# Rope moves of three query groups split over two DMA queues

## The chip, the core and the metric

The kernel runs on one core of a Trainium2 chip. The metric is the device time of one execution, in microseconds. A core has TensorE (PE in the profile), VectorE (DVE), ScalarE (ACT), GpSimd (POOL) and SyncE (SP); SyncE only issues DMAs here, and ScalarE can issue them too, from its own instruction stream.

## What is computed

Two layers over an input of 16 x 256 x 256 floats. Each layer normalises its input, computes a sequence mixer and a gate, and adds their product. In the first layer the mixer is a linear recurrence and the gate a feed-forward network. The second layer, in which the change lies, has attention with 16 heads and a routed low-rank gate:

```python
q = (x @ Wq).reshape(B, S, N_HEADS, QK_DIM)            # 128 nope + 64 rope
q = jnp.concatenate([q_nope, apply_rope(q_rope)], axis=-1)
kv = x @ Wkv_a                                         # 64 latent + 64 rope
c_kv = c_kv * rsqrt(mean(c_kv * c_kv) + RMS_EPS) * kv_norm_w
k = jnp.concatenate([k_nope, broadcast(apply_rope(k_rope))], axis=-1)
scores = jnp.einsum('bqhd,bkhd->bhqk', q, k) * scale
attn = softmax(where(tril, scores, min))
out = jnp.einsum('bhqk,bkhd->bqhd', attn, v) @ Wo
x = x + out * silu(routed_lora_ffn(xn))
```

The projection of the latent keys is folded into the queries' weights, so a head's key is the 64 latent numbers and the 64 rope numbers of a token, 128 partitions in all.

## The kernel before

The second layer works through 8 chunks of 512 tokens (two batch entries). A chunk has 4 groups of 4 heads, and each group is done once for each of the two batch entries: 8 units a chunk, 64 units in all. Unit `i` uses query group `i // 2`, and there are 32 groups. The order of the work is written out by hand, and a helper class (line 53, so that nearly every row of the profile has L53) keeps it on each engine.

*Scores.* `score_pack(u, 0..2)` multiplies the queries of a unit, `qg`, with the keys `kT` for eight blocks of 32 queries, in three packs that use three PSUM banks (`sc`) in turn. VectorE masks and takes the maxima, ScalarE takes the exponentials into `pr`, GpSimd divides by the sums (`normalise`).

*Probabilities.* They must be transposed before they meet the values. `turn` transposes them on VectorE in 32 x 32 blocks into `turned`; `send` writes them to a DRAM buffer `far` with four DMAs; one or two units later `fetch` reads them back as `pT` with one DMA. `far` and `pT` have three buffers each, `turned` two. `values(u)` multiplies `pT` with the latent rows into `av`, which ScalarE copies to `attT`.

*Queries.* While unit `i` runs, the queries of a group ahead are made: group `n = (i + 2) // 2` at even `i`, `(i + 3) // 2` at odd `i`. `query_mm` has four matmul steps into `pq`; `query_mul` (VectorE) and `query_rot` (GpSimd) apply the rotation and leave the result in `qrot`, which has one buffer; `query_lat` (ScalarE) writes the latent half, partitions 0 to 63, of `qg`. The rope half lies in `qrot` with the heads on the partitions and must come to partitions 64 to 127 of `qg`: `query_move(n)` does that with eight DMAs, two halves of the rotation by four heads, each of 32 partitions. `qg` has two buffers. The first score matmul of unit `2n` waits for all eight, and the next group's `query_rot` cannot write `qrot` before they are done.

*SyncE's queue.* `fetch`, `send` and `query_move` are all issued by SyncE, in the order of the program. At an even unit `i` that is `fetch(i - 2)`, then `send(i - 1)`, then `query_move(n)`; only at `i = 2` the moves stand ahead of the send. At an odd unit it is `fetch(i - 2)` and `send(i - 1)`. `fetch` waits for its `send` to have landed, so SyncE stands there for some time in every unit. [...]

*Last units.* The probabilities of the last two units do not go through DRAM: TensorE transposes them (`turn_here`).

In the loop, shortened to the calls that matter here:

```python
if 2 <= i:
    fetch(units[i - 2])
score_pack(u, 0)
...                       # turn(w, 1), turn(w, 2), query_mm, query_lat
score_pack(u, 1)
if i == 2:
    query_move(n)
turn(w, 0); send(w)       # w is unit i - 1
if not odd:
    if n is not None and i != 2:
        query_move(n)
    values(units[i - 4]); values(units[i - 3])
score_pack(u, 2)
...                       # odd: query_mm, query_mul, query_rot, query_lat
```

## Time and profile before

| | us |
|---|---|
| median of 3 runs | 921.33 (920.73 to 922.28) |
| profiled execution | 921.71 |
| its span | 919.9 |
| TensorE busy | 905.2 (98%) |
| VectorE busy | 666.4 (72%) |
| GpSimd busy | 570.6 (62%) |
| ScalarE busy | 465.8 (51%) |

The span is the time from the first to the last instruction in the profile, and the execution's own time holds it and what lies around it. The mean granted clock of TensorE over the execution was 0.996 of full speed. The attention layer begins at about 285 us and fills the rest. Over the whole execution SyncE issued 248 sends, 62 read-backs and 256 moves; in the profile they read `far<-turned`, `pT<-far` and `qg<-qrot`. Engine rows marked "q" (SPq, ACTq) are instructions that issue DMAs. A row of the timeline gives start, length, engine, line, operation, tiles and the number of instructions run together, and in brackets the idle time just before it with what ended it.

### The profile page before, as it was taken

To read this page: it belongs to the slowest core of one execution; us is meant where nothing else is said; L and a number is where in the kernel's file an instruction comes from. 1 tells how busy PE (TensorE), PEld (TensorE's weight loads), DVE (VectorE), ACT (ScalarE), POOL (GpSimd) and SP (SyncE) were. 2 spreads that over 40 slices of the span, in tenths; PEclk is the share of its full clock that TensorE was granted. 3 is DMA by queue.
4 is the path that set the end of the run, shared out by engine and by line. 5 is a ranking of instruction groups with operands and counts; after the bars stand their busy time and mean duration, and the time that the engine had idled before them with its cause. 6 is when DMAs were issued, how large, how long until landed. Compare 5 with 4: busy or idle time off the path is not lost.

```text
span 919.9 us, 17382 instructions
## 1 busy us (share of the span) xinstructions
PE 905.2 (98%) x5426; PEld 695.4 (76%) x5426; DVE 666.4 (72%) x2018; ACT 465.8 (51%) x1529; POOL 570.6 (62%) x885
## 2 busy tenths in 40 slices
PE   8999999999999899999999999999999999999998
PEld 7768898987767567777777777777777777777776
DVE  6876687664688779668967866896786689677562
ACT  3335555654336545645644564564466456446541
POOL 1228697777355537686586767648676764866541
PEclk9999999999999999999999999999999999999999
DMA  9730000000025777777776777777677777767771
GB/s 280 232 115 1 1 2 1 1 2 1 1 32 106 201 203 184 203 186 186 178 210 160 208 194 192 189 178 207 159 209 206 181 190 178 205 160 211 206 224 42
DMA packets 196412, 134.00 MB, mean 146 GB/s; under 512 B 142112, under 2 KB 186976, under 8 KB 196320
## 3 DMA queue, kind: packets, MB, share of 16 engines
q1 hardware_dynamic: 194192, 128.68, 53.3%
q0 software_dynamic: 1152, 3.67, 1.2%
q8 instruction: 44, 0.72, 0.3%
q10 hardware_dynamic: 976, 0.53, 0.2%
q14 instruction: 48, 0.39, 0.1%
HBM read 63.11 MB, written 52.95 MB: 126 GB/s over the span
## 4 chain that ended last, share of the span: by engine, by line
PE 90%; DVE 3%; DMA 2%; SPq 2%; POOL 1%; issue 1%; ACT 0%; POOLq 0%; DVEq 0%; ACTq 0%
PE pq L53 22%; PE sc L53 14%; PE po L53 10%; PE av L53 9%; PE r L53 7%; PE f L53 7%; PE ph L53 5%; PE pf L53 5%; PE pg L53 4%; PE pm L53 2%; SPq L53 2%; PE pkv L53 1%; PE tp L53 1%; DMA qg<-qrot 1%; PE py L53 1%; PE pb L53 1%
## 5 line engine op out<-in xcount | busy, mean ns | idle before, releaser
L53 ACT ACTIVATE pr<-sc,nm 128x256 f32<-128x256 f32 (+7 forms) x512 | 189.7, 381 | 240.3 <-DVE sr L53 152.2
L53 POOL TENSOR_SCALAR pr<-pr,sr 128x256 f32<-128x256 f32 (+7 forms) x512 | 192.1, 394 | 190.0 <-DVE sr L53 184.1
L53 PEld LDWEIGHTS sc<-kT,qg 128*128 128x128 f32 x1024 | 157.6, 191 | 62.3 <-issue 40.3
L53 PE MATMUL sc<-kT,qg 128*128 128x256 f32 (+7 forms) x1024 | 176.1, 306 | 5.7 <-DMA qg<-qrot 4.4
L53 DVE TENSOR_REDUCE nm<-sc 128x1 f32<-128x256 f32 (+7 forms) x512 | 127.5, 301 | 6.6
L53 DVE STREAM_TRANSPOSE turned<-pr 128x512 f32<-128x512 f32 x186 | 123.2, 687 | 9.6 <-POOL pr L53 8.7
L53 PE MATMUL pq<-xnT,wlat 128*128 128x512 f32 x256 | 124.1, 608 | 0.0
L53 PE MATMUL pq<-xnT,wrope 128*128 128x512 f32 x256 | 120.2, 593 | 0.0
L53 ACT ACTIVATION_READ_ACCUMULATOR pr<-sc,nm 128x1 f32 x512 | 104.3, 204 | 0.0
L53 DVE TENSOR_TENSOR sc<-sc,kmask 128x96 f32<-128x96 f32 (+1 forms) x192 | 45.5, 237 | 64.9 <-PE sc L53 63.9
L53 PE MATMUL av<-pT,row 128*64 128x256 f32 (+1 forms) x1024 | 90.9, 329 | 0.5 <-DMA pT<-far 0.5
L53 POOL TENSOR_TENSOR qrot<-qmul,qmul 128x512 f32<-128x512 f32 x64 | 83.0, 1317 | 8.0 <-POOL pr L53 2.9
L53 PEld LDWEIGHTS av<-pT,row 128*64 128x64 f32 x1024 | 64.1, 137 | 24.3 <-issue 1.6
L53 DVE TENSOR_TENSOR qmul<-pq,rot_q 128x512 f32<-128x512 f32 x128 | 80.7, 672 | 0.1
L53 ACT ACTIVATE qg<-pq 64x512 f32<-64x512 f32 x128 | 75.4, 589 | 5.4 <-PE pq L53 4.7
L53 PEld LDWEIGHTS pq<-xnT,wlat 128*128 128x128 f32 x256 | 46.0, 192 | 32.0 <-issue 32.0
L53 PEld LDWEIGHTS pq<-xnT,wrope 128*128 128x128 f32 x256 | 45.7, 191 | 32.4 <-issue 32.1
L53 PEld LDWEIGHTS po<-wout,attT 128*128 128x128 f32 x416 | 58.4, 191 | 9.5 <-issue 4.9
L53 PE MATMUL po<-wout,attT 128*128 128x128 f32 (+1 forms) x416 | 64.5, 308 | 0.0
L53 POOL TENSOR_TENSOR rs<-ve,mhalf 128x4 f32<-128x4 f32 (+1 forms) x17 | 16.8, 986 | 51.3 <-DVE ve L53 37.0
L53 PE MATMUL ph<-xnT,p1T 128*128 128x256 f32 (+1 forms) x128 | 44.3, 503 | 0.8 <-DVE xnT L53 0.8
L53 POOL TENSOR_TENSOR attT<-attT,attT 128x512 f32<-128x512 f32 x36 | 45.0, 1270 | 0.0
(226 smaller groups left out, 1505.0 us busy)
## 6 DMA issues: line engine op xcount, KB each, us to landing
far<-turned SPq DMA_DIRECT2D x248, 192.0 KB, 4.3
pT<-far SPq DMA_DIRECT2D x62, 768.0 KB, 5.0
qg<-qrot SPq DMA_DIRECT2D x256, 64.0 KB, 2.3
x<-in_x_dram SPq DMA_DIRECT2D x7, 512.0 KB, 9.3
out_dram<-x POOLq DMA_DIRECT2D x12, 256.0 KB, 4.9
wqn_wo<-in_wq_nopeT_dram SPq DMA_DIRECT2D x4, 512.0 KB, 4.9
wqn_wo<-in_Wo_dram SPq DMA_DIRECT2D x4, 512.0 KB, 6.1
p2T<-in_proj2T_dram SPq DMA_DIRECT2D x2, 512.0 KB, 7.2
```

What stands on the lines that cost most here:

```text
L53: r = getattr(self.engine, name)(*args, **kw)
```

## The change

At three units, `i` = 2, 4 and 60, the eight moves of a group (2, 3 and 31, that is the third, the fourth and the last) are taken from their place and split. The four moves of the first half are issued by SyncE at the start of the unit, in front of `fetch`. The four of the second half are issued by ScalarE, behind the exponentials of pack 1 and in front of whatever ScalarE does next. All other groups stay as they were.

```diff
-    def query_move(n):
+    def query_move(n, halves=(0, 1), e=sp):
         q = groups[n]
-        for r in range(2):
+        for r in halves:
             for h in range(G):
-                sp.dma_start(
+                e.dma_start(
                     q.qg[64 + 32 * r : 96 + 32 * r, :, h, :],
                     q.rot[32 * h : 32 * h + 32, r, :].rearrange("p (a q) -> p a q", q=32),
                 )
...
+    SOON = (2, 4, LAST - 4)
...
+        if i in SOON:
+            query_move(n, (0,))
         if 2 <= i:
             fetch(units[i - 2])
         score_pack(u, 0)
...
-        if i == 2:
-            query_move(n)
+        if i in SOON:
+            query_move(n, (1,), ac)
         if w:
...
         if not odd:
-            if n is not None and i != 2:
+            if n is not None and i not in SOON:
                 query_move(n)
```

## The prediction

> **What bounds the kernel now.** I read the page's busy shares first, then TensorE's waits, the timeline of each such wait, and SyncE's (SP's) queue ahead of it. The busy shares and TensorE's waits:

> ```profile
> PE 905.2 (98%) x5426; PEld 695.4 (76%) x5426; DVE 666.4 (72%) x2018; ACT 465.8 (51%) x1529; POOL 570.6 (62%) x885
> ```
> ```profile
> PE sc L53 <- DMA qg<-qrot: 4.4, 2, 3.5
> PE sc L53 <- ACT pr L53: 1.3, 1, 1.3
> PE av L53 <- DMA pT<-far: 0.5, 1, 0.5
> ```

> TensorE is the bound; in the attention layer it has few waits, and one of 3.5 us is the largest. On the timeline of TensorE (start, length, idle before it) these waits lie at three places that the change could touch, and a fourth that it leaves:

> ```profile
> 321.68 1.05 PE L53 MATMUL sc<-kT,qg 128*128 128x256 f32 x4 [3.47 <-DMA qg<-qrot]
> 322.57 3.35 PE L53 MATMUL pq<-xnT,wlat 128*128 128x512 f32 x4
> ...
> 881.40 1.87 PE L53 MATMUL sc<-kT,qg 128*128 128x256 f32 x10 [1.26 <-ACT pr L53]
> ...
> 885.24 1.52 PE L53 MATMUL av<-pT,row 128*64 128x256 f32 x16 [0.52 <-DMA pT<-far]
> ```

> The first is unit 6, which opens query group 3: its scores need the eight rope moves of that group, and the last landed at 321.27. The 881.40 row is unit 62, which opens group 31; the profile names ScalarE as releaser, but its exps were done at 880.86 and the last move of group 31 landed at 880.99, so it is the moves here too. 885.24 is values(59), released by its read-back. The fourth, 0.95 us at 380.60 (group 6), is left alone.

> Now SP's queue, which carries read-back (pT<-far), sends (far<-turned) and moves (qg<-qrot):

> ```profile
> 309.91 0.34 SPq L53 DMA_DIRECT2D pT<-far  x1
> 310.29 3.30 SPq L53 DMA_DIRECT2D far<-turned  x4
> 313.71 5.93 SPq L53 DMA_DIRECT2D qg<-qrot  x8
> 319.74 0.56 SPq L53 DMA_DIRECT2D pT<-far  x1
> ...
> 869.76 0.34 SPq L53 DMA_DIRECT2D pT<-far  x1
> 870.23 3.24 SPq L53 DMA_DIRECT2D far<-turned  x4
> 873.89 5.46 SPq L53 DMA_DIRECT2D qg<-qrot  x8
> 879.45 0.56 SPq L53 DMA_DIRECT2D pT<-far  x1
> ```

> Group 3's qrot was ready at 306.87 (GpSimd's timeline), yet its moves began at 313.71: SP was held until 309.9 by the landing of send(2), then issued a read-back and four sends. Group 31 likewise: ready at 866.22, moved from 873.89. Eight moves hold SP for 5.93 us, 0.63 us each, and land 2.3 us after issue (page, DMA issues). The queue's order makes the stall, not the transfers.

> **What the stall costs.** More than it shows. The granted clock in the stretch is below full:

> ```profile
> 301.00:318.00 17.00, 17.00 (x98) 11.30 (x96) 14.07 (x46) 9.83 (x40) 10.16 (x20) 1.00 0.77 225
> 318.00:341.00 23.00, 19.53 (x104) 13.16 (x104) 14.67 (x56) 10.01 (x37) 8.34 (x18) 0.93 0.75 188
> 341.00:361.00 20.00, 19.97 (x108) 14.21 (x108) 18.13 (x58) 13.24 (x54) 13.47 (x25) 1.00 0.72 172
> ```

> 0.93 over 23 us is one interval of 3.41 us at half speed (322.83 to 326.24), right behind the 3.47 us of idleness. The four pq matmuls there took 3.35 us; the same four take 1.96 at 316.25. With the six score matmuls behind them (1.25 instead of 1.08) that is about 1.6 us. [...]

> **The change, part by part.** At i = 2, 4 and 60 (groups 2, 3 and 31) four of eight moves go to the head of SP's queue, and four to ScalarE's queue behind pack 1's exps.

> *Removed from SP.* Four moves, 4 x 0.67 = 2.7 us of SP a site (interval of unhindered issues: 0.66 to 0.67). The other four run while SP used to wait: at i = 4 from 306.9, at i = 60 from 866.2.

> *Added to ScalarE.* Four issues a site. No row shows a move issued by ScalarE while it works. Below: its five issues of loads at the start, 0.33 to 0.48 us. Above: a move held up on SP, 1.24 us (at 314.34). I take 0.67, SP's interval for the same tile form, so 2.7 us a site. ScalarE then reaches pack 2's exps late: pack 1 ended at 307.93 (i = 4), pack 2 began at 309.27. Queued behind the moves are values' copy to attT (307.81, 0.6 us), pack 2's exps and one activation for the key/value chunk, and on them wait VectorE and GpSimd. ScalarE is 51% busy and the score ring is three banks deep, which hides the exps from TensorE; VectorE's work on the chunk moves from 310.6 to about 314.2, and the transposes behind it by up to 3.6 us.

> *i = 2.* SP's halves 290.0 to 292.6; ScalarE's from 295.4, landed about 300. fetch(0) goes from 290.98 to about 297.7 and lands by 303, needed at 304.9. fetch(1) goes from 303.0 to about 304.6, lands 309.5, needed at 311.6. Nothing gained or lost; the cover is 2 us.

> *i = 4.* ScalarE's moves 309.7 to 312.3 (behind the attT copy or the last exps), SP's by 314. qg_3 is complete at about 316; TensorE would want it at 318.05. **The stall and its clock dip go: 5.1 us, locally.** But fetch(2) slides from 309.91 to about 314.0, fetch(3) from 319.74 to 321.05, fetch(4) from 327.22 to 328.15, and send(5) stays at 328.8 against 328.73. So SP reaches group 4's moves when it did before, and they land at about 339.7 against 339.76. Unit 8 opens with them; in the trace it starts at 340.30, with TensorE free at 340.16. TensorE, now 5 us early, waits: 2.5 us at values(3), whose read-back lands at 326.2, and the rest at unit 8. **What remains of 5.1 us is what group 4's moves gain: 0.1 us at 0.67 us an issue, 1.3 us at 0.47.** I take 0.5.

> *i = 60.* SP's halves 865.2 to 870.3 (one waits for send(58)'s landing at 869.6), ScalarE's 869.8 to 872.4. fetch(58) slides from 869.76 to 872.15, but its probabilities are needed only at 883.2. Group 31 lands at about 875, so the 1.26 us at 881.40 go; fetch(59) goes at 879.25 instead of 879.45 and lands at 884.35 (5.1 us in flight), so values(59) starts at 884.45 against 885.24. **0.8 us**, with bounds 0.2 and 1.8 (1.26 + 0.52). This is near the end: no later move takes it back.

> Sum: 0.5 + 0.8 = **1.3 us**. The profiled execution took 921.71 us (span 919.9), which becomes 920.4; it lies 0.4 above the median of 921.33, which becomes **920.0**.

> [...] The row says 0.63 us of issue against 2.3 us of transfer, eight in a row: 5 us of a queue is not small. [...]

> **The rivals.** (0.2%, 1.84 us, is about what a measurement of this kernel can tell from no change.)

> *More is kept.* ScalarE issues in 0.47 us, or the moves land before SP looks for them, and group 4 comes 1.3 us earlier; with 0.8 to 1.3 at the end, 2.1 to 2.6 us: 919.0. For it: every issue that ScalarE has in this trace lies below 0.5. Against: those were into an idle chip. Were nothing given back, 5.1 + 1.8 = 6.9 us would be the most; unit 8's moves exclude that.

> *All is given back.* The read-backs slide, unit 8 takes all, values(59) keeps its time: 921.3. For it: 339.76 against 340.16 at group 4, and pT<-far releasing 885.24. Against: fetch(59) stood behind eight moves.

> *Slower: ScalarE's issues jam.* One mechanism: SP's fetch(2) waits for ScalarE's four moves, and SP's later issues slide with them. The four intervals count twice on the way to unit 8: in fetch(2)'s start, and in the exps and transposes behind the moves, on which send(5) waits. Eight intervals of 0.67 us leave unit 8 where it was, so it moves by 8 intervals less 5.4 us, an estimate. With 0.8 at the end, nothing is lost up to 0.77 us an issue, and 0.2% from about 1.0. At the jammed row's 1.24 us unit 8 is 4.5 us late, less 0.8: 3.7 us, 925.0. For it: far and pT packets fill the queues at 75% DMA share, and 1.24 to 1.61 us do occur. Against: they occur once in eight, not four times.

> **How the numbers follow.** Central case (0.4 to 1.84 us gained) 0.38; more kept 0.37; given back, within 0.4 us, 0.12; jam, 0.13 beyond 0.2%. Faster by over 0.2% is 'more kept' and a little of the central case, 0.39; within 0.2% 0.48; slower 0.13. The range runs from 918.3 (3 us gained: 1.3 with all of the end's 1.8) to 922.8 (a jam of 0.85 us an issue and noise of 0.9, the spread of the three runs); the jam's far end and a larger gain are left out, 2 in 10.

> **What would show it.** Right: no qg wait at unit 6 and clock 1.00 from 318 to 341; a new wait of 2 to 3 us at values(3), by pT<-far; unit 8 waiting on qg; SP's fetch(2) at about 314, waiting for a qg<-qrot landing; no wait at unit 62, and values(59) 0.8 us nearer the stage's start; ScalarE's moves about 0.67 us each. Wrong: a qg wait at unit 6 still there, ScalarE's moves at over 1 us, a half-clock interval at values(3) or unit 8 (one costs 1.6 us), or units after 8 that keep over 2 us.

## The result

The changed kernel took 925.76 us (median of 13 runs, 923.48 to 930.19) against 921.55 us (13 runs, 919.41 to 925.29) for the kernel before: ratio 1.0044, interval 1.0032 to 1.0056. It is 4 us slower where 1.3 us of gain were forecast. The execution that was profiled first, at 923.48 us, is the fastest of the 13, with a span of 921.7 us (before: 921.71 us and 919.9 us), so its trace shows 1.8 us of the 4. A second profiled execution of the same kernel, at 926.29 us, is nearer to the median; both are shown.

TensorE's waits, first profile, then the second:

```profile
PE av L53 <- DMA pT<-far: 5.1, 2, 3.1
PE sc L53 <- DMA far<-turned: 2.1, 1, 2.1
```
```profile
PE av L53 <- DMA pT<-far: 4.8, 2, 3.4
PE sc L53 <- DVE sr L53: 3.2, 1, 3.2
PE sc L53 <- DMA far<-turned: 1.8, 1, 1.8
```

The 4.4 us on qg<-qrot are gone, and in their place stand waits for read-backs and two new waits of scores. On TensorE's timeline, first profile:

```profile
303.16 1.05 PE L53 MATMUL sc<-kT,qg 128*128 128x256 f32 x4 [2.10 <-DMA far<-turned]
...
319.79 0.97 PE L53 MATMUL sc<-kT,qg 128*128 128x256 f32 x4
...
327.85 1.87 PE L53 MATMUL av<-pT,row 128*64 128x256 f32 x16 [3.10 <-DMA pT<-far]
...
881.75 1.79 PE L53 MATMUL sc<-kT,qg 128*128 128x256 f32 x10
...
887.01 1.52 PE L53 MATMUL av<-pT,row 128*64 128x256 f32 x16 [2.02 <-DMA pT<-far]
```

Unit 6 (319.79) and unit 62 (881.75) start without a wait: the moves do come early enough. But unit 4 (303.16) now waits 2.10 us, values(3) 3.10 us, and values(59) 2.02 us instead of 0.52. The releaser named at 303.16 is wrong: a score matmul needs no far<-turned. The trace has group 2's last move, on ScalarE's queue, landing at 302.73, and the name went to a send that landed beside it, at 303.17.

Where the time went, as the start of the same matmul in the two first profiles (each from its own span's start; differences of unrounded times):

| matmul | before | after | difference |
|---|---|---|---|
| unit 4, first score | 301.50 | 303.16 | +1.66 |
| unit 6, first score | 321.68 | 319.79 | -1.90 |
| unit 6, pack 1 (the half-clock stretch is gone) | 325.71 | 322.31 | -3.40 |
| values(3) | 328.24 | 327.85 | -0.39 |
| unit 8, first score | 340.30 | 343.10 | +2.79 |
| unit 62, first score | 881.40 | 881.75 | +0.35 |
| values(59) | 885.24 | 887.01 | +1.77 |

Between values(3) and unit 8 the changed kernel loses 3.2 us with no wait at all. The windows show why (the last three figures of a row are the granted clock, the busy share of the DMA engines and their GB/s):

```profile
318.00:324.00 6.00, 6.00 (x30) 3.77 (x31) 5.93 (x19) 3.92 (x17) 2.68 (x6) 1.00 0.68 212
324.00:332.00 8.00, 4.90 (x37) 3.98 (x34) 3.08 (x12) 3.73 (x12) 2.68 (x5) 0.80 0.67 220
332.00:345.00 13.00, 13.00 (x55) 9.53 (x55) 9.48 (x37) 4.67 (x20) 2.92 (x8) 0.86 0.77 208
```

The clock ran at half speed from 328.88 for 6.83 us (granted clock 0.50 up to 335.71), twice the 3.41 us of before; the sixteen pm matmuls there took 3.97 us instead of 2.10. In the second profile the half-clock stretch (granted clock 0.84 from 341 to 352) comes after unit 8, which there waits 3.20 us for group 4's moves:

```profile
344.62 1.56 PE L53 MATMUL sc<-kT,qg 128*128 128x256 f32 x4 [3.20 <-DVE sr L53]
```

The last of these moves landed at 344.07; the profile names VectorE. So the wait that left unit 6 turned up at values(3) and unit 8, and its clock loss came with it, once or twice over.

SyncE's and ScalarE's queues, first profile:

```profile
293.78 0.71 ACTq L53 DMA_DIRECT2D qg<-qrot  x1
294.53 0.64 ACTq L53 DMA_DIRECT2D qg<-qrot  x1
295.21 1.32 ACTq L53 DMA_DIRECT2D qg<-qrot  x2
```
```profile
289.39 2.61 SPq L53 DMA_DIRECT2D qg<-qrot  x4
296.18 0.35 SPq L53 DMA_DIRECT2D pT<-far  x1
...
310.18 4.20 SPq L53 DMA_DIRECT2D qg<-qrot  x4
314.49 0.55 SPq L53 DMA_DIRECT2D pT<-far  x1
315.09 2.26 SPq L53 DMA_DIRECT2D far<-turned  x4
322.95 0.34 SPq L53 DMA_DIRECT2D pT<-far  x1
```

The same queue before, at i = 2:

```profile
290.98 0.34 SPq L53 DMA_DIRECT2D pT<-far  x1
...
303.02 0.34 SPq L53 DMA_DIRECT2D pT<-far  x1
303.47 2.35 SPq L53 DMA_DIRECT2D far<-turned  x4
```

ScalarE's issues at i = 2 take 0.64 to 0.71 us, as assumed. The read-backs are late: fetch(0) at 296.18 instead of 290.98, fetch(2) at 314.49 instead of 309.91, fetch(3) at 322.95 instead of 319.74. Fetch(0) goes out 0.08 us after ScalarE's first move has landed (296.10); in the trace the two share a completion counter.

### The profile page after: what moved, and what is told of

Its sections match the earlier page's. It is cut to its first block, busy times and chain, and to the rows that moved or that the text cites. A ratio compares the mean times of both kernels' runs of the same rounds, so it can differ in the third digit from the quotient of the medians.

```text
span 921.7 us, 17371 instructions
## 1 busy us (share of the span) xinstructions
PE 906.0 (98%) x5426; PEld 697.6 (76%) x5426; DVE 665.8 (72%) x2018; ACT 466.0 (51%) x1529; POOL 570.8 (62%) x885
## 4 chain that ended last, share of the span: by engine, by line
PE 94%; DMA 3%; DVE 1%; SPq 0%; ACT 0%; issue 0%; POOL 0%; ACTq 0%; POOLq 0%
PE pq L53 23%; PE sc L53 15%; PE po L53 10%; PE av L53 9%; PE r L53 7%; PE f L53 7%; PE ph L53 5%; PE pg L53 5%; PE pf L53 5%; PE pm L53 2%; PE pkv L53 2%; PE tp L53 1%; DMA far<-turned 1%; DMA pT<-far 1%; PE py L53 1%; PE pb L53 1%
## 5 line engine op out<-in xcount | busy, mean ns | idle before, releaser
L53 POOL TENSOR_SCALAR pr<-pr,sr 128x256 f32<-128x256 f32 (+7 forms) x512 | 191.8, 393 | 190.6 <-DVE sr L53 184.4
L53 ACT ACTIVATE pr<-sc,nm 128x256 f32<-128x256 f32 (+7 forms) x512 | 189.8, 381 | 233.1 <-DVE sr L53 145.9
L53 PEld LDWEIGHTS sc<-kT,qg 128*128 128x128 f32 x1024 | 158.5, 192 | 57.8 <-issue 40.9
L53 PE MATMUL sc<-kT,qg 128*128 128x256 f32 (+7 forms) x1024 | 176.8, 307 | 2.2 <-DMA far<-turned 2.1
L53 DVE TENSOR_REDUCE nm<-sc 128x1 f32<-128x256 f32 (+7 forms) x512 | 127.7, 301 | 6.6
L53 DVE STREAM_TRANSPOSE turned<-pr 128x512 f32<-128x512 f32 x186 | 123.4, 688 | 9.4 <-POOL pr L53 9.2
L53 PE MATMUL pq<-xnT,wlat 128*128 128x512 f32 x256 | 122.7, 602 | 0.0
L53 PE MATMUL pq<-xnT,wrope 128*128 128x512 f32 x256 | 120.2, 593 | 0.0
L53 ACT ACTIVATION_READ_ACCUMULATOR pr<-sc,nm 128x1 f32 x512 | 104.4, 204 | 0.0
L53 PE MATMUL av<-pT,row 128*64 128x256 f32 (+1 forms) x1024 | 91.5, 330 | 5.1 <-DMA pT<-far 5.1
L53 DVE TENSOR_TENSOR sc<-sc,kmask 128x96 f32<-128x96 f32 (+1 forms) x192 | 45.8, 238 | 62.6 <-PE sc L53 61.4
L53 POOL TENSOR_TENSOR qrot<-qmul,qmul 128x512 f32<-128x512 f32 x64 | 83.5, 1324 | 7.1 <-DVE qmul L53 2.8
L53 PEld LDWEIGHTS av<-pT,row 128*64 128x64 f32 x1024 | 64.3, 137 | 29.2 <-DVE turned L53 3.3
L53 DVE TENSOR_TENSOR qmul<-pq,rot_q 128x512 f32<-128x512 f32 x128 | 80.9, 674 | 0.1
L53 ACT ACTIVATE qg<-pq 64x512 f32<-64x512 f32 x128 | 75.4, 589 | 4.3 <-PE pq L53 3.5
L53 PEld LDWEIGHTS pq<-xnT,wrope 128*128 128x128 f32 x256 | 45.7, 191 | 32.4 <-issue 32.1
L53 PEld LDWEIGHTS pq<-xnT,wlat 128*128 128x128 f32 x256 | 45.7, 191 | 31.6 <-issue 31.6
L53 PEld LDWEIGHTS po<-wout,attT 128*128 128x128 f32 x416 | 58.4, 191 | 9.5 <-issue 5.1
L53 PE MATMUL po<-wout,attT 128*128 128x128 f32 (+1 forms) x416 | 64.5, 308 | 0.0
L53 POOL TENSOR_TENSOR rs<-ve,mhalf 128x4 f32<-128x4 f32 (+1 forms) x17 | 16.8, 986 | 51.0 <-DVE ve L53 37.3
L53 POOL TENSOR_TENSOR attT<-attT,attT 128x512 f32<-128x512 f32 x36 | 45.0, 1270 | 0.0
L53 PE MATMUL ph<-xnT,p1T 128*128 128x256 f32 (+1 forms) x128 | 44.1, 501 | 0.8 <-DVE xnT L53 0.8
```

The source lines that it names most:

```text
L53: r = getattr(self.engine, name)(*args, **kw)
```

## The experiments

Each difference is against the changed kernel. "Undone" means that a group goes as in the kernel before.

**The changed kernel again**, no edit.

> The changed kernel once more, for a second profile. In its first profile the span grew by 1.8 us, put together from: 2.1 us of wait at unit 4 (group 2's last move on ScalarE's queue landed at 302.7), minus the 3.5 us wait of unit 6, plus 3.1 us at values(3) (read-back) and a half-clock interval of 6.8 us instead of 3.4 us, minus 1.3 us at unit 62 and 1.5 us more at values(59). Theory (three places add up, and each is as deterministic as the queue order): the same waits in the same places, each within 0.5 us, time 925 to 927. Rival (the median's 4 us is something the first profile did not catch): other or larger waits than these.

Measured: ratio 1.0040 (1.0025 to 1.0056), median 925.71 us. The waits of unit 4 (1.78) and values(3) (3.35) lie within 0.4 us of the first profile, that of values(59) (1.43) is 0.6 us shorter. Unit 8's 3.20 us are new, and the final shift is 4.6 us instead of 1.8. The other places are as in the first profile, but the size of the wait at unit 8 and the place of the half-clock stretch differ from execution to execution, and that is what the first profile did not catch.

**One site at a time.**

```diff
-    SOON = (2, 4, LAST - 4)
+    SOON = (2,)              # only_third
+    SOON = (4,)              # only_fourth, group 2 undone
+    SOON = (LAST - 4,)       # only_last, group 2 undone
```

> Only the third group (i = 2) is split over the queues; groups 3 and 31 go as in the kernel before. Theory A: the last ScalarE move lands with the read-back's packets at about 302.7, unit 4 waits 2.1 us, SyncE's queue is 1.6 us later from then on, unit 6 keeps its wait of 3 to 3.5 us: plus 1.6 to 2.5 us, 923 to 924. Theory B: the 2.1 us are absorbed by the wait of unit 6, which shrinks to about 1.5 us: 921 to 921.8.

> Only the fourth group (i = 4) is split; group 2 goes whole in front of the send as in the kernel before, group 31 in its old place. Theory A: without the 1.7 us that unit 4 brings along, fetch(3) goes out at about 321 and values(3) waits 2 to 2.5 us, one half-clock interval or none, unit 8 within 1 us of before: 920.3 to 922. Theory B: the loss lies here whatever group 2 does: values(3) waits 3 us, two half-clock windows, 923.5 to 925.

> Only the last group (i = 60) is split. Theory A (the read-back of unit 59 is later because fetch(58) stood behind ScalarE's moves): the 1.3 us at unit 62 go, values(59) waits 1.5 to 2 us more: plus 0 to 0.5 us, 921.3 to 922. Theory B (as forecast, once the queue does not come late from earlier units): minus 0.8 us, 920.7.

Measured: only_third 1.0040 (1.0028 to 1.0052), only_fourth 1.0015 (1.0002 to 1.0028), only_last 0.9990 (0.9976 to 1.0004). **The third group alone, the site I had costed at nothing, loses about as much as all three changes together** (1.0040 against 1.0044); with the fourth group's 1.0015 the parts don't add up place by place, since in the whole change unit 6 no longer waits for a late group 3. In only_third unit 4 waits 1.92 us, and unit 6 waits on top of that what it waited before:

```profile
303.10 1.05 PE L53 MATMUL sc<-kT,qg 128*128 128x256 f32 x4 [1.92 <-DMA far<-turned]
...
323.23 1.94 PE L53 MATMUL sc<-kT,qg 128*128 128x256 f32 x4 [3.34 <-DMA qg<-qrot]
```

so theory B, that unit 6's wait would absorb it, falls: group 3's moves come later by the same amount. The loss of 3.7 us is more than theory A's 1.6 to 2.5: the profiled execution also had a longer half-clock stretch (the three groups of matmuls from 323.23 to 329.58 took 1.94, 3.62 and 1.28 us; at full speed they take 0.97, 1.88 and 0.98). Of its 3.7 us, 1.6 stand at unit 4 and 1.7 come between units 4 and 20, where that stretch is. In only_fourth the stall of unit 6 is gone, but values(3) waits 3.71 us and unit 8 another 1.85: the waits are those of theory B, with one half-clock stretch instead of its two windows (2.58 and 1.42 us for two groups of matmuls that take 1.52 and 0.85 at full speed, and full speed again at 331.41).

**The third group, three ways.**

```diff
 # third_sync_only: the second half on SyncE, at the same place
-            query_move(n, (1,), ac)
+            query_move(n, (1,))
 # third_read_first: fetch in front of SyncE's half
+        if 2 <= i:
+            fetch(units[i - 2])
         if i in SOON:
             query_move(n, (0,))
-        if 2 <= i:
-            fetch(units[i - 2])
 # third_three: ScalarE issues heads 1 to 3 alone; query_move takes the heads too
-    def query_move(n, halves=(0, 1), e=sp):
+    def query_move(n, halves=(0, 1), e=sp, heads=range(G)):
...
             query_move(n, (0,))
+            query_move(n, (1,), sp, (0,))
...
-            query_move(n, (1,), ac)
+            query_move(n, (1,), ac, (1, 2, 3))
```

All three with `SOON = (2,)`.

> Only the third group is split in time, as in only_third, but the second half is issued by SyncE too, at the same place of the program (behind fetch(0), in front of the send). Theory A: the moves follow the read-back in one queue, so fetch(0) waits for nobody and goes out at 292; the last move lands at about 299; unit 4 has no wait: 921 to 922. Theory B (taking SyncE's first halves in front of the read-back is what costs): unit 4 or unit 6 waits more than before, 923 to 925.

> Only the third group is split, as in the run only_third, but at i = 2 the read-back fetch(0) is issued in front of SyncE's four moves instead of behind them; ScalarE still issues the other four. Theory A (the 4 us of only_third come from ScalarE's last move and a read-back being issued at the same moment, 295.9 and 296.2 us, so that the move lands with the read-back, 6.7 us later): fetch(0) goes out at about 290, no move is issued beside it, ScalarE's moves land 2.3 us after issue, unit 4 has no wait, 921 to 922. Theory B (a move on ScalarE's queue is slow in itself, or it delays ScalarE): unit 4 waits again, 923.5 to 925.5.

> Only the third group is split, as in only_third, but ScalarE issues three moves instead of four and SyncE five at the head of unit 2. Theory A (the read-back starts when ScalarE's first move has landed, 2.3 us after its issue; three issues of 0.68 us are done by then, four are not, and the one in the making lands with the read-back): all three land 2.3 us after issue, unit 4 has no wait, the 2.1 us go; 921.5 to 923. Theory B (moves on ScalarE's queue land late because of the traffic of that moment, however many they are): the last lands with the read-back again at about 302.5, unit 4 waits about 2 us, 924 to 926.

Measured: third_sync_only 0.9998 (0.9985 to 1.0011), third_read_first 1.0009 (0.9995 to 1.0022), third_three 1.0024 (1.0011 to 1.0036). Third_three settles what happens at unit 4. ScalarE's three moves all land 2.2 to 2.4 us after issue (the fourth of only_third took 6.68, landing 0.24 us after the read-back that SyncE issued 0.29 us behind it), and unit 4 has no wait. But the kernel is still 2.4 parts in a thousand slower, outside theory A's time: fetch(0) waits for ScalarE's first move as before (landed at 296.35, fetch(0) at 296.42), and unit 6 now takes all of it:

```profile
324.25 1.94 PE L53 MATMUL sc<-kT,qg 128*128 128x256 f32 x4 [6.48 <-DMA qg<-qrot]
```

So the late move at unit 4 is only where the loss first shows. Its root is SyncE's chain: from unit 4's first score (301.06), fetch(1) goes out 3.34 us later and fetch(2) 10.63 us later, where before these were 1.52 and 8.41. With the second half on SyncE (third_sync_only) the read-back doesn't wait for ScalarE:

```profile
289.63 2.61 SPq L53 DMA_DIRECT2D qg<-qrot  x4
292.40 0.50 SPq L53 DMA_DIRECT2D pT<-far  x1
292.94 2.73 SPq L53 DMA_DIRECT2D qg<-qrot  x4
295.78 4.33 SPq L53 DMA_DIRECT2D far<-turned  x4
302.74 0.34 SPq L53 DMA_DIRECT2D pT<-far  x1
```

and no loss can be measured: fetch(1) is at 302.74 (before: 303.02). The early half is harmless at i = 2; SyncE's wait for ScalarE is not. Third_read_first lies between: fetch(0) goes out in time and unit 4 doesn't wait, but SyncE's fourth move goes out at 298.77, once ScalarE's first has landed (298.76), so that four moves hold the queue for 7.17 us, and unit 6 waits 4.38 us.

```profile
292.19 7.17 SPq L53 DMA_DIRECT2D qg<-qrot  x4
```

**The fourth group, three ways.**

```diff
 # fourth_read_first: fetch in front of SyncE's half, as above
 # fourth_sync_head: all eight at the head, on SyncE
-            query_move(n, (0,))
+            query_move(n)
...
-            query_move(n, (1,), ac)
 # fourth_gpsimd: all eight on GpSimd at the later place, none at the head
-            query_move(n, (0,))
...
-            query_move(n, (1,), ac)
+            query_move(n, (0, 1), gp)
```

All three with `SOON = (4,)` and group 2 undone.

> Only the fourth group is split, as in only_fourth, but fetch(2) stands in front of SyncE's four moves. Theory A (only_fourth loses because fetch(2) waits for ScalarE's moves, 314.5 instead of 309.9, and every later read-back and send slides by 3 us): fetch(2) at 309.9, fetch(3) at about 320, group 3 complete before 318, no wait at unit 6, at most 1 us at values(3), unit 8 as before: 920 to 921.3. Theory B (ScalarE's own late exps and copies, which hold VectorE's transposes for 3.6 us, cost the time): unit 8 or values(3) waits over 2.5 us again, 922.5 to 924.

> Only the fourth group is changed: all eight moves are issued by SyncE at the head of unit 4, none by ScalarE. Theory A (the loss is the order of SyncE's queue, whichever engine issues the moves): fetch(2) slides to about 312.5, fetch(3) to 320.5 or later, values(3) waits 1 to 2 us, unit 8 about as before: 920.5 to 922. Theory B (ScalarE's share is the loss): no wait over 1 us at values(3) and unit 8, 919.5 to 920.5.

> Only the fourth group is changed: all eight moves are issued by GpSimd at unit 4, behind the normalising of pack 2; SyncE and ScalarE issue none of them, and GpSimd's DMAs have completion counters of their own. Theory A (the time lost at i = 4 is all in SyncE's chain of read-back, send and read-back, which moves in front of it or on shared counters push back): fetch(2) stays at 309.9, send(3) lands by 317.5, fetch(3) goes out at 317.5 instead of 319.7, group 3 is complete by about 317, unit 6 and values(3) wait less than 1 us together, unit 8 comes 1 to 4 us earlier: 917.5 to 920. Theory B (the transfers themselves, in whatever queue, or GpSimd's issuing at over 1 us each, are the limit): unit 6 or values(3) waits over 2 us, 921 to 923.

Measured: fourth_read_first 1.0006 (0.9994 to 1.0017), fourth_sync_head 1.0001 (0.9987 to 1.0014), fourth_gpsimd 1.0003 (0.9991 to 1.0016). None gains. To compare the executions, times are counted here from unit 4's first score matmul, in us:

| kernel | fetch(2) | fetch(3) | group 3 landed | unit 6 | values(3) | unit 8 |
|---|---|---|---|---|---|---|
| before | 8.41 | 18.24 | 19.77 | 20.18 | 26.74 | 38.80 |
| only_fourth | 12.05 | 20.40 | 13.47 | 16.55 | 25.22 | 40.81 |
| fourth_read_first | 10.21 | 19.81 | 17.01 | 17.14 | 25.09 | 40.38 |
| fourth_sync_head | 11.19 | 19.82 | 12.82 | 16.55 | 25.05 | 39.22 |
| fourth_gpsimd | 8.58 | 19.42 | 17.93 | 18.06 | 24.34 | 39.58 |

Unit 6 comes 2 to 3.6 us earlier in each, and unit 8 in none. These are single executions. In four others, in which SyncE alone issues groups 2 and 3 and group 3 has its old place (third_sync_only, only_last, only_last_again, last_sync_only), fetch(3) lies at 18.28 to 18.44 and unit 8 at 38.73 to 39.71. So fetch(3) is late in all four changed kernels, by 1.2 to 2.2 us, whoever issues the moves, but unit 8 is clearly later only in the two with moves on ScalarE. And unit 8 isn't earlier where the half-clock stretch is missing: only_last has none (its four pq matmuls at 322.53 take 1.88 us, 3.35 before), and there unit 8 waits 1.40 us and starts at 38.73 all the same.

With moves on ScalarE the counters delay fetch(2). In only_fourth and fourth_read_first the last part of send(2) shares a counter with fetch(1) and goes out only when fetch(1) has landed (308.83 after 308.82; 307.59 after 307.57). In only_fourth the send takes 4.81 us to issue instead of 2.35, and SyncE's moves start behind it:

```profile
304.33 4.81 SPq L53 DMA_DIRECT2D far<-turned  x4
309.41 4.81 SPq L53 DMA_DIRECT2D qg<-qrot  x4
```

In fourth_read_first that part lands at 311.33 and fetch(2) follows at 311.35. So its lateness is no case of theory B, ScalarE's late exps.

Fourth_gpsimd takes the moves out of SyncE's queue and off its counters, and fetch(2) is on time. (GpSimd's DMAs have counters of their own: in the trace of before its 16 use eight that no DMA of SyncE or ScalarE uses. The eight of the prediction are shared by SyncE and ScalarE, not by all engines.) Yet send(3) lands late all the same, since fetch(2) took 8.14 us to land instead of 5.05, and GpSimd's moves 6.7 us (median) instead of 2.3. Their issues took 0.65 to 0.91 us, not over 1. The waits, 1.35 us at unit 6 and 1.24 at values(3), fit neither theory; the time fits theory B. The profiled execution, 925.24 us, was the slowest of its twelve (median 922.88). The DMA issues of that kernel, in the window from 303 to 325:

```profile
pT<-far SPq DMA_DIRECT2D x3, 768.0 KB, 5.0
far<-turned SPq DMA_DIRECT2D x12, 192.0 KB, 5.2
qg<-qrot POOLq DMA_DIRECT2D x8, 64.0 KB, 6.7
```

**DMAs in flight together landed later in these runs (that fetch(2) 8.14 us after its issue instead of 5.05), and the moves are no small matter there.** In the changed kernel ScalarE's queue (q10) is nearly a meter for them. Its row in the DMA queues of the whole execution, before and after:

```profile
q10 hardware_dynamic: 976, 0.53, 0.2%
q10 hardware_dynamic: 7312, 1.32, 0.8%
```

So twelve moves cost 0.6% of 921.7 us, an estimate of 0.46 us of all 16 engines each (from rounded shares), 3.7 us for a group. That is what the packets took, not a measured delay of what stands behind them: fetch(3) came 1.2 to 2.2 us late. GpSimd's queue (q0) packs the same bytes otherwise, eight moves in 256 packets where ScalarE's take 528 each:

```profile
q0 software_dynamic: 1152, 3.67, 1.2%
q0 software_dynamic: 1408, 4.20, 1.5%
```

(before, then fourth_gpsimd). So that run shows that moves from another queue hold up a read-back, not what a move on SyncE's queue costs. Nor is the delay a constant: a read-back with moves close behind it in SyncE's queue took 5.28 us (fourth_read_first), 5.44 (before, i = 2), 6.44 (third_sync_only) and 8.00 (last_sync_only). What decides is open.

In the old order the moves ran in the shade of a send that had to land anyway: send(3) landed at 316.9, moves were issued from 313.71 to 319.64, fetch(3) followed at 319.74.

Theory B of fourth_read_first has some room still behind fetch(2): unit 8 is later (40.81 and 40.38) in both kernels with moves on ScalarE than in fourth_sync_head (39.22). ScalarE's late exps and the counters are not separated there.

**The last group.**

```diff
 # last_sync_only: SOON = (LAST - 4,), group 2 undone, second half on SyncE
-            query_move(n, (1,), ac)
+            query_move(n, (1,))
```

> Only the last group (i = 60) is split in time: first half in front of fetch(58), second half behind it and in front of the send, all eight issued by SyncE. Theory A (the gain of only_last comes from the order alone; the read-backs have slack there): unit 62 has no wait, fetch(58) goes out at about 870.5 by the clock of before, values(59) is no later: ratio 0.998 to 0.9995. Theory B (the gain needs the second queue): unit 62 or values(59) waits as before or longer: 0.9995 to 1.002.

> The run only_last once more, beside last_sync_only, for a narrower interval and a second profile. If its gain is real: minus 0.5 to 1.2 us, unit 62 without a wait, values(59) waiting 1 to 1.5 us. If it was noise: within 0.3 us of before.

Measured: last_sync_only 1.0028 (1.0011 to 1.0046), only_last_again 1.0014 (1.0000 to 1.0028). With only_last's 0.9990 the two runs of the same kernel lie on either side of no change; its effect on the whole isn't resolved, and it isn't shown to beat the kernel before. Locally both profiles look like the forecast: against before, unit 62 starts 1.4 us sooner after unit 61, and values(59) gives 0.68 and 0.28 us of it back. But that is not shown to be the change: from unit 60's first score to values(59) it takes 20.69 and 20.22 us here, 21.43 before, and 20.05 to 21.92 in the eight other profiles that leave group 31 in place. The rows of the first:

```profile
879.25 1.79 PE L53 MATMUL sc<-kT,qg 128*128 128x256 f32 x10
...
883.69 1.52 PE L53 MATMUL av<-pT,row 128*64 128x256 f32 x16 [1.20 <-DMA pT<-far]
```

Last_sync_only goes against theory A, and its time lies beyond theory B's range: here the second queue does help. Part of the loss is a half-clock stretch at values(59): its sixteen av matmuls took 2.83 us instead of 1.52. With SyncE alone, four moves follow fetch(58) closely, fetch(58) takes 8.0 us to land, send(59) stretches over 5.16 us, and values(59) waits 3 us longer than before:

```profile
870.78 0.34 SPq L53 DMA_DIRECT2D pT<-far  x1
871.47 3.48 SPq L53 DMA_DIRECT2D qg<-qrot  x4
875.04 5.16 SPq L53 DMA_DIRECT2D far<-turned  x4
883.06 0.34 SPq L53 DMA_DIRECT2D pT<-far  x1
```
```profile
888.09 2.83 PE L53 MATMUL av<-pT,row 128*64 128x256 f32 x16 [3.57 <-DMA pT<-far]
```

The opposite of i = 2, where SyncE alone was the harmless way: there fetch(1) went out when it did before, while here fetch(59), which has no slack, went out at 883.06 instead of 879.45.

## Why the prediction was wrong

*"The queue's order makes the stall, not the transfers."* This sentence failed. The order does make the wait at unit 6, and changing it removes that wait (all five kernels that move group 3 ahead show it smaller or gone). But moves put elsewhere push other DMAs, by their transfers as well as by their counters: in fourth_gpsimd a read-back beside moves from another queue took 8.14 us, 5.05 without. My row of 0.63 us of issue against 2.3 us of landing answered a different question: 2.3 us is a median, not what a move costs its neighbours. The trace of before already had it: the eight moves of group 2, right behind fetch(0), took from 5.39 down to 2.41 us to land.

*i = 2, "nothing gained or lost".* This step failed: taken alone it costs 3.7 us (only_third, 1.0040). I had fetch(0) at 297.7 and fetch(1) at 304.6; they came at 296.18 and 304.60. The agreement of the second is luck: fetch(0) went out 1.5 us sooner, and the last part of the send behind it flew 6.0 us instead of the 3.5 of before. And I checked both against their own consumers alone. Two terms were missing. A move that ScalarE had just issued as SyncE's read-back started landed with it, at 302.73 beside 302.49 instead of at "about 300", which is unit 4's wait; and the 1.6 us by which fetch(1) slid go on through fetch(2) to group 3's moves, which had no slack at all while they stood in their old place. Third_three shows the second alone.

*i = 4, "what remains is what group 4's moves gain".* The stall and its half-clock stretch went, and fetch(2) came at 314.49 against the 314.0 forecast, though not by the wait I named alone: a part of send(2), held until fetch(1) had landed (309.59 after 309.57), moved SyncE's half from 306.9 to 310.18, and its fourth move then waited for ScalarE's second (313.80 after 313.78). The step that failed is the next: fetch(3) at 321.05 was 322.95 (322.84 in only_fourth). I had let send(3) fly as long as in the trace of before, some 4.7 us; behind a read-back and four moves it took 6.2. From there values(3) waited 3.1 to 3.7 us instead of 2.5, fetch(4) and group 4's moves slid too, and unit 8, which I had as 0.5 us early, was 2.8 us late in the first profile and 4.3 in the second. The half-clock stretch, counted as gone, came back at values(3) or unit 8; the one of before cost 1.6 us, and I named this as what would make the forecast wrong without giving it a place in the sum.

*The clock.* The 5.1 us of i = 4 are the 3.47 us of the stall and the 1.6 us that its half-speed stretch cost. I took the second to go with the first, from the one stall in the trace of before. The runs show that the two can part: in only_last unit 6 waits 3.68 us and the clock stays full (four pq matmuls in 1.88 us, 3.35 in before), and in the first profile of the changed kernel, with no wait at unit 6, 3.10 us at values(3) are followed by 6.83 us at half speed. So the 1.6 us were not certain to be there.

*i = 60, 0.8 us.* The two profiles of only_last fit it locally, 1.4 less 0.7 and 1.4 less 0.3, but within the spread of kernels without the change. With all three changed, values(59) gave back 1.50 in the first profile and 0.91 in the second: a gain of about 0 to 0.5.

*The rivals.* The slower one gave nearly the right time, 925.0, by the wrong mechanism: no jam. ScalarE's issues stayed at 0.6 to 0.8 us but for the odd one of 0.84 to 1.47 (one of 2.38 in only_fourth). What was right in it was the place: SyncE's read-backs sliding behind ScalarE's moves.

## What to carry to other kernels

Charge a DMA that is moved ahead in a queue to what stands behind it as transfer time, not only as issue time, until the chain meets a wait with slack; in these runs a second issuing queue did not lift that charge (fourth_gpsimd's read-back at 8.14 us instead of 5.05). When one queue alternates "write out, read back", look for the gap in which the queue waits for the write to land: here no other place that was tried for the moves made the kernel measurably faster. In front of the read-back they cost nothing at i = 2 (all on SyncE) and delayed the next read-back at i = 4. And where completion counters are shared, a DMA put on another engine can make the first engine wait for it, as fetch(0), issued at 296.18, waited for ScalarE's move that landed at 296.10; look at the built order of the counters, and follow the delay to the next consumer without slack, not just to the next one.

## What the runs showed of the hardware

A 64 KB move issued 0.29 us ahead of a 768 KB read-back on another queue landed 6.7 us after its issue, with the read-back, while its three predecessors took 2.2 to 2.3 us (only_third). From unit 4 to unit 8 the 14 profiles have fifteen waits of 2.91 to 6.48 us on TensorE: twelve were followed by matmuls at half speed, and three were not (only_last, 3.68 us at unit 6; last_sync_only, 3.55 at unit 6; all_three_again, 3.35 at values(3)). Of the shorter waits there, up to 2.10 us (unit 4 of the changed kernel, unit 8 of last_sync_only), none was.

The half-speed stretch was 3.41 us long in before (granted clock 0.50 from 322.83 to 326.24) and cost 1.6 us by the rows of its matmuls; in the changed kernel it was 6.83 us (0.50 from 328.88 to 335.71). What decides whether a wait is followed by one, and why the stretch is longer in some executions, is open. These stretches are part of the spread between runs of one kernel: over the 112 executions of the kernel before that were timed beside the experiments, time and mean granted clock correlate by -0.49, about a quarter of the variance.

The releaser that a profile named was a DMA on which the instruction cannot depend (far<-turned at 303.16, unit 4) or an engine that had long been done (VectorE at 344.62, unit 8): the landing times of the moves there, 302.73 and 344.07, told the true one.
